# A GRU in sum-product form on one core: biases by DMA, first step's input products in scratch banks, last group's products made plainly

## The chip, the cores and the metric

One core of a Trainium2 chip runs the whole kernel. The metric is the device time of one execution in microseconds (us). The times below are medians; the profile is of one execution, with its own time. A difference of about 0.2% is what this measurement can tell from none.

## The reference

The input x has 64 sequences of 128 steps and 512 features; the state h starts from a second input (64 x 512). Cut to what matters:

```python
def step(h, inp):
    x_t, prop = inp
    comb = jnp.concatenate([x_t, h], axis=-1)
    z = jax.nn.sigmoid(comb @ Wz + bz)
    r = jax.nn.sigmoid(comb @ Wr + br)
    comb2 = jnp.concatenate([x_t, r * h], axis=-1)
    h_cand = jnp.tanh(comb2 @ Wh + bh)
    h_new = (1.0 - z) * h + z * h_cand
    h_next = jnp.where(prop, jnp.tanh(h_new @ Wp + bp), h_new)
    return (h_next, h_new)
...
x = x + ys        # ys: all the h_new
```

`prop` holds at every fourth step but the last. All is float32. Each gate's weight matrix has 512 rows for x_t (`wx` in the kernel) and 512 for h (`wh`).

## The kernel before, in words

**Layout.** The 64 sequences and two halves of the 512 features fill the 128 partitions: a state tile is 128 x 256 (`N` = 256), with half s on partitions 64s to 64s+63. A product with a 512 x 512 matrix is four calls of `product` (L196), one for each block k of 128 input features, each with one matmul for each half s (L187). A trace lists four records for one call. The activations, transposed for use as the stationary operand, come from `turn` (L205): four bf16 transposes on TensorE (L212), then one copy to SBUF on VectorE or ScalarE (L203).

**The recurrence.** One pass of the loop from L569 is a step: four products of h for R, four for Z; sigmoid of R, times h (`rh`, L602); `rh` transposed; Z's sigmoids and `keep` (L618); four products of `rh` for the candidate H; tanh, L648 and L653 to the new h; h transposed (L660, L662). At a chunk's end (`prop`) four products with Wp, a tanh and another transpose follow. The gates' PSUM slots (`slots`, in the tiles `rc` and `zp`) are seeded beforehand by ScalarE copies (`seed`, L392) with the input products and the bias of that step, which lie in `G`.

**The input products.** They do not depend on h and serve as fillers. A list `queue` holds single products; `fill(n)` (L400) issues the next n of them between the recurrence's own, and `read_out` (L407) issues the readers of those finished. How many go where is fixed by hand in `PLACES` (L537) and the numbers in the loop, by position u in a cycle of eight steps. Steps 0 to 7 are made plainly (`plain`, L411: 12 products a step, in two of the four scratch banks `q`, `r`, `a`, `x`, read by two VectorE additions with the bias, L419 and L424). From step 8 on, groups of four steps are made by a two-level fast matrix product (seven products of sums, each made of seven products of sums): 49 units a group of 128 x 192, in batches of two times seven (`batch`, L437), with sums of x and the final additions on GpSimd (L495, L499, L333 to L361) and reads by ScalarE and VectorE (L460 to L470). Two groups of 49 units are queued every eight steps (`batches`, L483). The weights' sums are made once, at the start: `sum_inner` (L318), `sum_outer` (L308), and in place in `wx` by L316 and L324. So `wx` no longer holds the plain weights later on, except in block k = 3. The last groups are 30 and 31 (steps 120 to 127).

**The start.** Each bias is loaded as a row to one partition (L109) and spread by matmuls with a row of ones (`spread`, L158) into `rc` and `zp`, from where VectorE copies it to `bias` (L168). `idle` (L177) issues matmuls of zeros. Then step 0's input products go straight to the gates' slots, with those of step 1 in between (L551 to L564).

**The queues.** TensorE, VectorE, ScalarE and GpSimd each take their instructions in program order. Loads are issued from SP's queue, some of the first ones from ScalarE's. A load may have to wait, on its issuing queue, for an earlier load's landing.

The functions that the diff touches, with the profile's line numbers:

Of the kernel before, what the change touches and what calls it, by code (L numbers as in the profile page):

```python
# [17 lines left out]
def kernel(  # L18
# [39 lines left out]
    FIRST = 2  # L58
    R, Z, H_ = range(3)
# [26 lines left out]

    bias_row = tt.rearrange("p a b c d e -> p (a b c d e)")[0:1, : 4 * H].rearrange(
        "p (i n) -> p i n", i=4
    )

# [17 lines left out]
    for i, b in enumerate((br, bh, bz, bp)):  # L108
        nc.scalar.dma_start(out=bias_row[:, i, :], in_=b.rearrange("(o n) -> o n", o=1))  # L109
    h_init = two.tile([P, N], F32, tag="h", name="h_init")  # L110
    new_xr(0)
    load_x(xr[0], 0, 2)
    for i in range(3):
        for k in (0, 2):
            load_w(wx[:, :, i, :], gates_in[i], k, k + 2, nc.sync if k == 0 else nc.scalar)
        if i == 0:
            for s in range(S):
                nc.scalar.dma_start(out=h_init[s * B : (s + 1) * B, :], in_=h0[:, ts(s, N)])
    for i in range(3):
        for k in (0, 2):  # L120
            load_w(wh[i], gates_in[i][D:, :], k, k + 2, nc.sync)
        if i == 0:
            load_x(xr[0], 2, 2, 2)
# [29 lines left out]
    bias = const.tile([P, C, 4, P], F32, name="bias")  # L153
# [3 lines left out]

    def spread(a, ps):  # L158
        for s in range(S):
            nc.tensor.matmul(  # L160
                ps[s * B : (s + 1) * B, :, :],
                lhsT=ones,
                rhs=bias_row[:, 2 * a : 2 * a + 2, ts(s, N)],
                start=True,
                stop=True,
            )
        for i in ((R, H_), (Z, 3))[a]:
            nc.vector.tensor_copy(bias[:, :, i, :], cut((slots[i] if i < 3 else slot_p)))  # L168
# [8 lines left out]
    def idle(n):  # L177
        for _ in range(n):
            nc.tensor.matmul(  # L179
                scratch[0][:B, :], lhsT=zeros[:, :B], rhs=zeros, start=True, stop=True  # L180
# [253 lines left out]

    MB = {}

    def batch(n, ms):  # L437
# [10 lines left out]
        def units(ps, j, start):  # L448
            return [lambda m=m: unit(ps, m, j, start) for m in range(2)]
# [4 lines left out]
        def end_1():  # L454
            MB[n] = mbp.tile([P, 2, 2, 3, P], F32, tag="mb", name=f"mb_{ms[0][0]}_{ms[0][1]}")
            for m, (g, i) in enumerate(ms):
                M[g, i] = MB[n][:, m]
            T2[n] = one.tile([P, 2, 3, P // 2], F32, tag="cx", name=f"cx_{ms[0][0]}_{ms[0][1]}")
            q1 = one.tile([P, 2, 3, P // 2], F32, tag="cq", name=f"cq_{ms[0][0]}_{ms[0][1]}")
            nc.scalar.copy(T2[n], x_ps)  # L460
            nc.scalar.copy(q1, q_ps)
            nc.vector.tensor_add(T2[n], r_ps, T2[n])  # L462
            nc.vector.tensor_add(blocks()[:, :, 0, 0], a_ps, q1)

        def end_2():
            q2 = one.tile([P, 2, 3, P // 2], F32, tag="cq", name=f"cq2_{ms[0][0]}_{ms[0][1]}")
            nc.scalar.copy(q2, q_ps)  # L467
            nc.vector.tensor_add(blocks()[:, :, 0, 1], r_ps, q2)  # L468
            nc.vector.tensor_add(blocks()[:, :, 1, 0], x_ps, q2)
            nc.vector.tensor_add(blocks()[:, :, 1, 1], q_ps, T2[n])  # L470
# [5 lines left out]
        seq[7] = (seq[7][0], end_1)  # L476
        seq[13] = (seq[13][0], end_2)
# [5 lines left out]
    def batches(g):  # L483
# [3 lines left out]
        ms = [(g, i) for i in (1, 2, 6, 5, 7, 3, 4)] + [(g + 1, i) for i in (1, 6, 2, 5, 3, 7, 4)]  # L487
        return sum((batch((g, n), ms[2 * n : 2 * n + 2]) for n in range(7)), [])
# [8 lines left out]
    def with_bias(g, i, v):  # L497
        m = M[g, i].rearrange("p b g u -> p b (g u)")
        nc.gpsimd.tensor_add(  # L499
            m, m, v.rearrange("p g u -> p (g u)").unsqueeze(1).to_broadcast([P, 2, 3 * P])  # L500
# [31 lines left out]
    def outer_c21(g):  # L532
# [7 lines left out]


    idle(10)
    spread(0, rc)
    turn_x(0, nc.vector)
    turn_x(1, nc.vector)
    spread(1, zp)
    nc.gpsimd.tensor_sub(bias_d, bias[:, 1, 0:3, :], bias0)
    idle(2)
    h = h_init
    hT = new_T("hT", "hT_init")  # L550
    first = [  # L551
        [lambda e=e, k=k: product(slots[e], xT[0][:, 0], wx[:, :, e, :], k) for k in ORDER]
        for e in range(3)
    ]
    second = plain(1)
    for e in range(3):

        queue.extend(second[4 * e : 4 * e + 4])
# [236 lines left out]
```

## Time and profile before

| | us |
|---|---|
| median of 3 runs | 1363.82 (1363.69 to 1363.88) |
| the profiled execution's own time | 1362.82 |
| its span, first to last instruction | 1361.0 |
| TensorE idle between 20 and 1300 us, by the waits | 2.7 |
| TensorE idle from 1300 us on, by the waits | 8.4 |

Of the chain that ended last, 98% lies on TensorE. Data moved by DMA in the first stretches, and the granted TensorE clock (1.00 is full):

| us | GB/s | share of DMA engines | clock |
|---|---|---|---|
| 2 to 4 | 133 | 0.61 | 1.00 |
| 4 to 6 | 250 | 0.91 | 1.00 |
| 6 to 8 | 398 | 1.04 | 1.00 |
| 8 to 10 | 346 | 1.06 | 1.00 |
| 10 to 11 | 331 | 1.09 | 0.74 |
| 12 to 13 | 385 | 1.05 | 0.50 |
| 13 to 14 | 385 | 1.05 | 0.55 |
| 14 to 15 | 387 | 1.06 | 1.00 |
| 20 to 25 | 318 | 1.09 | 1.00 |
| 25 to 30 | 267 | 1.10 | 1.00 |

How to read the rows quoted below. A row of the order of instructions gives start, duration, engine, line, operation, output and input tiles, shape and count; in brackets stands the idle time of the engine before it and what ended that. Matmul ends are modelled and overlap, so distances between starts tell more than durations. A row by windows gives the window, its length, the busy time and count of PE, PEld, DVE, ACT and POOL, then the granted clock, the share of the DMA engines and GB/s.

### The profile page before, as it was taken

The page shows a single profiled execution, that of the slowest core. Times are in us where ns is not written, and L with a number is a line of the kernel's source. Part 1 is how long each engine was busy: PE and PEld are TensorE (multiplying, and loading weights), DVE is VectorE, ACT ScalarE, POOL GpSimd, SP SyncE. Part 2 cuts the span into 40 slices and gives each one's busy share as a digit, 9 for nine tenths or more (in the row PEclk, how much of TensorE's full clock was granted, in tenths as well). Part 3 has the DMA queues.
Part 4 walks back from the last instruction along what each step waited for, and adds up shares of the span by engine and source line. Part 5 has one row for each costly group of instructions (what it writes and reads, how often), then busy time and mean ns, then how long its engine had stood idle before and what let it go on. Part 6 is the DMA issues. An engine that isn't in the chain of part 4 may idle for free.

```text
span 1361.0 us, 37468 instructions
## 1 busy us (share of the span) xinstructions
PE 1341.8 (99%) x15348; PEld 1033.1 (76%) x15348; DVE 686.0 (50%) x1875; ACT 630.6 (46%) x1857; POOL 935.7 (69%) x1140
## 2 busy tenths in 40 slices
PE   9999999999999999999999999999999999999996
PEld 6877777777777777777777777777777777777764
DVE  3255555555555555555555555555554555555543
ACT  1234544444544544444445444545445445444443
POOL 3448776778667768676787767777676686767740
PEclk9999999999999999999999999999999999999999
DMA  9011223121221222213222221222212212131010
GB/s 287 13 33 34 62 49 78 32 58 39 64 63 33 63 48 48 64 33 78 49 45 52 63 64 33 63 36 60 63 32 64 59 37 63 41 71 33 17 33 16
DMA packets 113572, 73.86 MB, mean 54 GB/s; under 512 B 61556, under 2 KB 109812, under 8 KB 113400
## 3 DMA queue, kind: packets, MB, share of 16 engines
q1 hardware_dynamic: 112336, 69.68, 22.6%
q8 instruction: 121, 1.98, 0.6%
q10 hardware_dynamic: 1064, 1.78, 0.4%
q14 instruction: 51, 0.42, 0.1%
HBM read 39.99 MB, written 16.78 MB: 42 GB/s over the span
## 4 chain that ended last, share of the span: by engine, by line
PE 98%; DVE 1%; ACT 0%; issue 0%; POOL 0%; DVEq 0%; POOLq 0%; ACTq 0%
PE rc L187 33%; PE zp L187 20%; PE scratch_q L187 11%; PE scratch_x L187 11%; PE scratch_r L187 10%; PE scratch_a L187 6%; PE turn L212 6%; PE scratch_q L179 0%; DVE h L653 0%; DVE turn L648 0%; ACT z L616 0%; PE rc L160 0%; ACT turn L647 0%; ACT xT L203 0%; ACT zp L617 0%
## 5 line engine op out<-in xcount | busy, mean ns | idle before, releaser
L187 PE MATMUL rc<-wh,rhT 128*64 128x256 f32 x2048 | 246.6, 381 | 2.0 <-ACT zp L617 2.0
L495 POOL TENSOR_TENSOR cp<-mb,mb 128x768 f32<-128x768 f32 x75 | 136.4, 1819 | 112.8 <-ACT rc L394 67.6
L187 PEld LDWEIGHTS rc<-wh,rhT 128*64 128x64 f32 x2048 | 158.9, 137 | 54.5 <-ACT zp L617 12.4
L187 PE MATMUL rc<-wh,hT 128*64 128x256 f32 x1536 | 183.1, 380 | 0.5 <-DVE hT L203 0.2
L187 PE MATMUL zp<-wh,hT 128*64 128x256 f32 x1536 | 183.2, 379 | 0.0
L203 DVE COPY rhT<-turn 128x256 uint16<-128x256 uint16 x256 | 96.7, 420 | 126.1 <-PE turn L212 126.1
L495 POOL TENSOR_TENSOR cp<-mb 128x768 f32<-128x768 f32 x45 | 81.9, 1819 | 108.2 <-ACT rc L394 107.0
L648 DVE TENSOR_TENSOR turn<-turn,z 128x128 f32<-128x128 f32 x256 | 75.5, 295 | 159.7 <-ACT turn L647 159.7
L187 PEld LDWEIGHTS zp<-wh,hT 128*64 128x64 f32 x1536 | 117.5, 137 | 47.3
L729 POOL TENSOR_TENSOR xr<-xr,h 128x256 f32<-128x256 f32 x127 | 92.8, 731 | 86.2 <-DVE h L653 85.2
L187 PEld LDWEIGHTS rc<-wh,hT 128*64 128x64 f32 x1536 | 111.6, 137 | 44.9 <-issue 1.0
L601 ACT ACTIVATE turn<-rc 128x128 f32<-128x128 f32 x256 | 55.4, 261 | 155.3 <-issue 84.2
L462 DVE TENSOR_TENSOR cx<-scratch_r,cx 128x384 f32<-128x384 f32 x105 | 58.6, 558 | 128.3 <-ACT cx L460 128.3
L203 ACT COPY hT<-turn 128x256 uint16<-128x256 uint16 x127 | 47.3, 373 | 155.8 <-PE turn L212 96.6
L495 POOL TENSOR_TENSOR mb<-mb,mb 128x768 f32<-128x768 f32 x60 | 109.4, 1824 | 14.2 <-DVE mb L470 14.2
L468 DVE TENSOR_TENSOR mb<-scratch_r,cq 128x384 f32<-128x384 f32 x105 | 58.6, 558 | 91.0 <-ACT cq L467 91.0
L394 ACT COPY rc<-cp 128x256 f32<-128x256 f32 x254 | 95.6, 376 | 11.6 <-POOL s L335 0.4
L616 ACT ACTIVATE z<-zp 128x256 f32<-128x256 f32 x128 | 49.2, 384 | 102.7 <-PE zp L187 100.8
L647 ACT ACTIVATE turn<-rc 128x128 f32<-128x128 f32 x256 | 56.7, 261 | 76.2 <-PE rc L187 76.2
L212 PEld LDWEIGHTS <-h 128*64 128x64 bf16 x1016 | 47.7, 109 | 50.5 <-DVE h L653 45.7
L394 ACT COPY zp<-cp 128x256 f32<-128x256 f32 x127 | 47.8, 377 | 74.5 <-DVE keep L618 74.5
L212 PE MATMUL turn<-ident,h 128*64 128x128 bf16 x1016 | 76.7, 227 | 5.4 <-DVE h L653 5.4
(152 smaller groups left out, 2960.4 us busy)
## 6 DMA issues: line engine op xcount, KB each, us to landing
xr<-in_x_dram SPq DMA_DIRECT2D x62, 256.0 KB, 4.2
out_dram<-xr SPq DMA_DIRECT2D x62, 256.0 KB, 3.4
xs<-in_x_dram SPq DMA_DIRECT2D x56, 256.0 KB, 4.3
wh<-in_L_cond_Wr_dram SPq DMA_DIRECT2D x2, 512.0 KB, 7.5
wh<-in_L_cond_Wz_dram SPq DMA_DIRECT2D x2, 512.0 KB, 8.9
wh<-in_L_cond_Wh_dram SPq DMA_DIRECT2D x2, 512.0 KB, 11.4
early<-in_x_dram SPq DMA_DIRECT2D x4, 256.0 KB, 13.4
wp<-in_L_cond_Wp_dram SPq DMA_DIRECT2D x1, 1024.0 KB
```

What stands on the lines that cost most here:

```text
L187: nc.tensor.matmul(ps[s * B : (s + 1) * B], lhsT=lhs, rhs=rhs(s), start=start, stop=True, skip_group_check=True,)
L203: (eng.copy if eng is nc.scalar else eng.tensor_copy)(dst, src)
L212: nc.tensor.transpose(pt[s * B : (s + 1) * B, w, :], words.rearrange("p (n w) -> p w n", w=2)[:, w, :], ident16,)
L394: nc.scalar.copy(cut(slots[i]), G[t][:, :, i, :])
L462: nc.vector.tensor_add(T2[n], r_ps, T2[n])
L468: nc.vector.tensor_add(blocks()[:, :, 0, 1], r_ps, q2)
L495: nc.gpsimd.tensor_add(dst, a, b)
L601: nc.scalar.activation(act_ps[c], slots[R][:, ts(c, P)], AF.Sigmoid)
L616: nc.scalar.activation(z, slots[Z], AF.Sigmoid)
L647: nc.scalar.activation(pc, slots[H_][:, ts(c, P)], AF.Tanh)
L648: nc.vector.tensor_mul(pc, pc, z[:, ts(c, P)])
L729: nc.gpsimd.tensor_add(xr[g][:, j, :], xr[g][:, j, :], h_new)
```

## The change

- The four biases are loaded by DMA on all 128 partitions (eight loads of 64 rows, in a layout by gate); the rows, the spreading matmuls and their copies go. Two of the loads come after the input weights on SP, the other two after the first weights for h.
- The first two steps of x are loaded in two halves, one as the first load on SP, the other as the first on ScalarE's queue. The initial state is loaded last on ScalarE's queue.
- `idle` makes fewer matmuls (6, 2 and 2 instead of 10 and 2), alternating between the halves of the partitions.
- Step 0's input products are made like those of step 1, in scratch banks, read with the bias and seeded into the slots.
- In step 3 the sums `sum_inner(5)` move from the end of the step to behind `keep`.
- Group 31 is made plainly: `plain_last` gives 48 products, and `reload` brings the overwritten blocks of the input weights back by nine loads at the end of step 118. All GpSimd work for group 31 goes. From step 119 on (`thin`), `TAIL` says how many fillers go where: none ahead of the candidate's products; two of Z's four products go behind the transposes of `rh`.

```diff
+    LAST = T // Q4 - 1
...
-    for i, b in enumerate((br, bh, bz, bp)):
-        nc.scalar.dma_start(out=bias_row[:, i, :], in_=b.rearrange("(o n) -> o n", o=1))
...
-    load_x(xr[0], 0, 2)
+    for s in range(S):
+        (nc.sync, nc.scalar)[s].dma_start(
+            out=xr[0][s * B : (s + 1) * B, 0:2, :], in_=x[:, 0:2, ts(s, N)]
+        )
     for i in range(3):
         for k in (0, 2):
             load_w(wx[:, :, i, :], gates_in[i], k, k + 2, nc.sync if k == 0 else nc.scalar)
-        if i == 0:
+    for s in range(S):
+        nc.scalar.dma_start(out=h_init[s * B : (s + 1) * B, :], in_=h0[:, ts(s, N)])
+
+    def load_bias(gates):
+        for i in gates:
             for s in range(S):
-                nc.scalar.dma_start(out=h_init[s * B : (s + 1) * B, :], in_=h0[:, ts(s, N)])
+                nc.sync.dma_start(
+                    out=bias_in[s * B : (s + 1) * B, i, :],
+                    in_=(br, bz, bh, bp)[i][ts(s, N)]
+                    .rearrange("(o n) -> o n", o=1)
+                    .broadcast_to([B, N]),
+                )
+
+    load_bias((0, 1))
     for i in range(3):
         for k in (0, 2):
             load_w(wh[i], gates_in[i][D:, :], k, k + 2, nc.sync)
         if i == 0:
+            load_bias((2, 3))
             load_x(xr[0], 2, 2, 2)
...
-    bias = const.tile([P, C, 4, P], F32, name="bias")
+    bias = bias_in.rearrange("p i (c n) -> p c i n", c=C)
...
+    def idle(n):
+        for i in range(n):
+            s = i % S
             nc.tensor.matmul(
-                ps[s * B : (s + 1) * B, :, :],
-                lhsT=ones,
-                rhs=bias_row[:, 2 * a : 2 * a + 2, ts(s, N)],
+                (rc, zp)[i // S % 2][s * B : (s + 1) * B, :, :],
+                lhsT=zeros[:, :B],
+                rhs=zeros,
                 start=True,
                 stop=True,
...
+    def plain_last():
+
+
+        def units(t, gates, first_k):
+            first, second = scratch[:2] if t % 2 == 0 else scratch[2:]
+            regions = (first[:, :N], first[:, N:], second[:, :N])
+            return [
+                lambda e=e, k=k: product(
+                    regions[e], xT[LAST][:, t % Q4], wx[:, :, e, :], k, k == 3 and e != Z
+                )
+                for k in first_k
+                for e in gates
+            ]
...
+        t0 = LAST * Q4
+        seq = [(u, None) for t in (t0, t0 + 1) for u in units(t, (R, Z, H_), (3,))]
+        for t in (t0, t0 + 1):
+            us = units(t, (R, Z, H_), (1, 0, 2))
+            seq += [(u, None) for u in us[:-1]] + [(us[-1], lambda t=t: end(t, (R, Z, H_)))]
+        for t, gates in ((t0 + 2, (R, Z, H_)), (t0 + 3, (R, Z)), (t0 + 3, (H_,))):
+            us = units(t, gates, (3, 1, 0, 2))
+            seq += [(u, None) for u in us[:-1]] + [(us[-1], lambda t=t, g=gates: end(t, g))]
+        return seq
+
+    def reload():
+
+        for k in (1, 0, 2):
+            for i in range(3):
+                load_w(wx[:, :, i, :], gates_in[i], k, k + 1, nc.sync)
...
-        ms = [(g, i) for i in (1, 2, 6, 5, 7, 3, 4)] + [(g + 1, i) for i in (1, 6, 2, 5, 3, 7, 4)]
-        return sum((batch((g, n), ms[2 * n : 2 * n + 2]) for n in range(7)), [])
+        ms = [(g, i) for i in (1, 2, 6, 5, 7, 3, 4)]
+        if g + 1 < LAST:
+            ms += [(g + 1, i) for i in (1, 6, 2, 5, 3, 7, 4)]
+        return sum((batch((g, n), ms[2 * n : 2 * n + 2]) for n in range(7) if 2 * n < len(ms)), [])
...
-        m = M[g, i].rearrange("p b g u -> p b (g u)")
+        m = M[g, i]
         nc.gpsimd.tensor_add(
-            m, m, v.rearrange("p g u -> p (g u)").unsqueeze(1).to_broadcast([P, 2, 3 * P])
+            m, m, v.unsqueeze(1).to_broadcast([P, 2, 3, P])
         )
...
-    idle(10)
-    spread(0, rc)
+    TAIL = (
+        ((4, 1, 0), (2, 1)), ((4, 1, 0), ()), ((4, 1, 0), ()), ((4, 1, 0), ()),
+        ((4, 1, 0), (2, 1)), ((4, 1, 0), ()), ((5, 1, 2), ()), ((3, 1, 0), ()), ((0, 0, 0), ()),
+    )
+
+
+    idle(6)
     turn_x(0, nc.vector)
+    idle(2)
     turn_x(1, nc.vector)
-    spread(1, zp)
+    idle(2)
...
+    both = [plain(0), plain(1)]
     for e in range(3):
-
-        queue.extend(second[4 * e : 4 * e + 4])
-        for n in range(4):
-            first[e][n]()
-            fill(1)
-        if e == 0:
+        for us in both:
+            queue.extend(us[4 * e : 4 * e + 4])
+        fill(4)
+        if e == H_:
+            read_out()
+            seed(R, 0)
+            seed(Z, 0)
+            seed(H_, 0)
+        fill(4)
+        if e == Z:
...
+        thin = t >= T - 9
+        if thin:
+
+            places, behind = TAIL[t - (T - 9)]
+            if t == T - 9:
+                assert not queue
+                queue.extend(plain_last())
+        if t == T - 10:
+
+            places = (4, 6)
+            assert len(queue) == 7
...
+        if t == T - 1:
+            seed(H_, t)
...
-        for k in ORDER[: 2 if last else K]:
+        for k in ORDER[: 2 if thin else K]:
             product(slots[Z], hT, wh[Z], k)
         rhT = new_T("rhT", f"rhT_{t}")
         for c in range(C):
             turn(rh, rhT, c, f"rhT_{t}", nc.vector)
-        if last:
-            for k in ORDER[2:]:
-                product(slots[Z], hT, wh[Z], k)
+            if thin:
+                product(slots[Z], hT, wh[Z], ORDER[2 + c])
...
         nc.vector.tensor_mul(keep, slots[Z], h)
+        if t == 3:
+            sum_inner(5, nc.vector)
+            sum_inner_1(5, nc.vector)
         seed(Z, t + 1)
...
-        fill(places[0])
+        if not thin:
+            fill(places[0])
...
-        fill(places[1] - 3 if places[1] > 6 else 4)
+        fill(places[0] if thin else places[1] - 3 if places[1] > 6 else 4)
...
-            fill(1)
+            fill(places[1] if thin else 1)
             turn(h, hT, 1, f"hT_{t}", nc.scalar)
-        fill(2 if places[1] > 6 else 1)
+        fill(places[2] if thin else 2 if places[1] > 6 else 1)
...
+        if t == T - 10:
+            reload()
```

## Prediction

> **What bounds the kernel now.** I read the page first, then busy time cut at the step boundaries (each step's first `rc<-wh,hT` matmul), then the order of instructions in the three places with idle TensorE: the start, step 3 and the end.
>
> ```profile
> span 1361.0 us, 37468 instructions
> ...
> PE 1341.8 (99%) x15348; PEld 1033.1 (76%) x15348; DVE 686.0 (50%) x1875; ACT 630.6 (46%) x1857; POOL 935.7 (69%) x1140
> ```
>
> TensorE is the bound nearly throughout. Its busy time is drawn out by pipelining, so I cost work by start-to-start distances: sixteen 128x256 records (four `product` calls) start 1.735 us before what follows them, so a product takes 0.434 us; a sum-product unit of 128x192 takes 0.325 (four records, 1258.12 to 1258.45); eight transposes 0.22. From about 108 to 1313 us nothing stops TensorE, and its work per step there is not changed. So only the start, step 3 and the tail count. The tail, by step (122, 123, 124, 127):
>
> ```profile
> 1303.63:1313.52 9.89, 9.71 (x117) 7.55 (x113) 5.60 (x15) 4.30 (x14) 6.42 (x5) 1.00 0.01 2
> 1313.52:1325.04 11.52, 8.88 (x89) 6.12 (x89) 4.91 (x14) 4.78 (x16) 6.20 (x5) 1.00 0.13 26
> 1325.04:1333.48 8.44, 6.46 (x64) 4.14 (x65) 2.99 (x10) 2.77 (x11) 0.40 (x1) 1.00 0.09 29
> ...
> 1350.35:1361.00 10.65, 5.77 (x56) 3.80 (x56) 2.76 (x9) 1.84 (x7) 1.06 (x2) 0.89 0.21 51
> ```
>
> The queue of input products runs dry in step 122; from 123 on the matmul count falls to 64 and each step is pure latency. Inside step 124:
>
> ```profile
> 1329.44 1.95 PE L187 MATMUL rc<-wh,rhT 128*64 128x256 f32 x16 [0.51 <-ACT zp L617]
> 1332.53 0.31 PE L212 MATMUL turn<-ident,h 128*64 128x128 bf16 x4 [1.14 <-DVE h L653]
> 1333.06 0.31 PE L212 MATMUL turn<-ident,h 128*64 128x128 bf16 x4 [0.22 <-DVE h L653]
> 1333.48 1.95 PE L187 MATMUL rc<-wh,hT 128*64 128x256 f32 x16
> ```
>
> The candidate product ends at 1329.44 + 1.735 = 1331.17; the state is back for its transpose 1.36 later and the next step starts 0.95 after that. 2.31 us hang on DVE and ACT; fillers there are free.
>
> **Part 1, the tail.** The last group's 49 sum-product units (49 x 0.325 = 15.9 us) become 48 plain products (48 x 0.434 = 20.8), 4.9 us more TensorE work, spread over steps 119 to 126 as 8, 5, 5, 5, 8, 5, 8 and 4. In these steps two Z products go behind the transposes of `rh`, in the form the last step already has. There R start to H start is 1350.35 to 1354.23 = 3.88 us, against 4.40 unfilled (1333.48 to 1337.88). H takes 1.735. Then four fillers (1.735) replace the 1.36 wait; the next step starts about 0.93 after the first transpose, because the copy on DVE (0.41) is then the last to come, and one 0.434 filler fits in it. A five-filler step is 3.88 + 1.735 + 1.735 + 0.03 + 0.93 = 8.3 us, as long as a step with none (8.44). By step, before against after: 118 (seven old units left, none between the transposes) 8.55, 9.1; 119 (with the 1.735 of the chunk-end product, two fillers and 0.84 from its transpose to the next step) 14.09, 11.8; 120 and 121 8.43, 8.44 against 8.3 each; 122 9.89, 8.3; 123 11.52, 11.8; 124 8.44, 8.3; 125 8.44, 9.4; 126 8.43, 7.9. Sums 86.2 and 83.3: **2.9 us gained**, and 127 as before. The ends: 4.9 if the transposed copy is ready when TensorE is (0.25 in each of eight steps), 0.2 if thinner Z cover costs 0.3 in each of nine steps. If the cover were gone altogether, the fillers would cost their 4.9.
>
> The nine reloads of the input weights (256 KB each, 2.36 MB) go on SP behind the load for group 30 and ahead of the output of step 119. No row shows this load alone. Near rows: 385 GB/s at the start with loads abreast, so 6 us; or 4.2 us for one 256 KB load, nine in a row 38 us. The first six products use the block that needs no reload, so the first reloaded piece is wanted late in step 119, the last at the end of 120, about 20 us after the issue. I take the abreast value: nothing. DVE reads of the plain products (four times 0.68 + 0.42 us) run under the R products of the following step; the removed reads and GpSimd additions (1.8 us each) weren't on the path.
>
> **Part 2, step 3.**
>
> ```profile
> 84.22 1.95 PE L187 MATMUL zp<-wp,hT 128*64 128x256 f32 x16
> 85.40 0.55 DVE L324 TENSOR_TENSOR wx<-wx 128x384 f32<-128x384 f32 x1
> 85.87 0.55 DVE L468 TENSOR_TENSOR mb<-scratch_r,cq 128x384 f32<-128x384 f32 x1
> 86.80 0.55 DVE L470 TENSOR_TENSOR mb<-scratch_q,cx 128x384 f32<-128x384 f32 x1
> 87.40 0.55 PE L187 MATMUL scratch_q<-tw,o 128*64 128x192 f32 x4 [1.23 <-DVE mb L470]
> ```
>
> TensorE was free at 84.22 + 1.735 = 85.96. The DVE reads that release the scratch bank stood behind the four `sum_inner(5)` operations (83.75 to 85.95). The change puts these four behind `keep`, where DVE was idle from 78.31 to 80.45; four at about 0.55 fill 2.2 us, and the next read comes at most 0.1 late, under the H products. The bank's reads then wait for ACT's copy (84.11 to 84.60) and end near 86.15: the stall shrinks from 1.44 to 0.2, **1.2 us gained**. Ends: 1.4, and 0 if the four take longer than here. The stalls at 94.24 and 104.57 (0.5 and 1.0 on DVE `rh`, behind ACT copies) stay.
>
> **Part 3, the start.**
>
> ```profile
> 7.77 2.68 SPq L98 DMA_DIRECT2D wh<-in_L_cond_Wr_dram  x2
> 9.50 1.07 PE L160 MATMUL zp<-tt,ones 1*64 1x512 f32 x4
> 10.51 0.69 PE L187 MATMUL rc<-wx,xT 128*64 128x256 f32 x1
> 13.49 0.59 PE L187 MATMUL rc<-wx,xT 128*64 128x256 f32 x1
> 25.15 1.89 PE L187 MATMUL zp<-wh,hT_init 128*64 128x256 f32 x15
> ```
>
> Removed: two `spread` pairs on TensorE (1.43 and 1.07 us), four DVE copies of 0.42, four row loads. The first x half lands 2.8 us after its issue, the other is issued 0.7 later on the same queue and lands after some 5; on two queues both should land near 3.5, not 6.6. The first wx load lands 5.6 after its issue, at 7.8; its queue comes to it 0.75 sooner, so I put it at 7.0. The x transposes end before (3.6 to 5.3, with 0.76 of DVE copies behind each). So products start at 7.0 instead of 10.51. The same 24 products follow, now in scratch banks for both steps; the DVE additions and ACT seeds that this adds for step 0 (0.69 + 0.42, then 0.38 each) lie under the last four products (1.735). If all else kept its distance (10.51 to 25.15, 14.64 us), step 0's Z products would start at 21.6.
>
> Two things hold that back. First the clock. The row: products take twice their later time until 13.49, three us after their start, although ten zero matmuls had run from 1.90 to 6.37. [...]
>
> Second the weights. A load waits for an earlier one's landing: the first wh load was held 3.9 us for wx. In the changed order both wh_R loads wait for the last wx halves, and eight bias loads of 64 KB (0.52 MB, 1.4 us at the 385 GB/s of 12 to 16 us) stand on SP ahead of and behind them, then x, then wh_Z. Summing from 3.5 MB moved near 12.7 us: wh_R lands near 17.4, wanted near 20.7; six issues of 0.65 bring wh_Z to 17.5 and its landing to about 22, under 22.7. With SP's later pace (1.3 MB from 17.6 to 22.5, 267 GB/s) it is 24.8. **2.4 us gained** (25.15 - 22.7); ends 0.3 and 3.8. GpSimd's `bias_d` waits for the bias of the candidate (11.15 before, near 19 now), and behind it nine `sum_inner` operations of 1.05; they had 7.3 us of waiting for DVE after them, which covers it. `with_bias` reads the bias in another layout, 1.83 us each; no row shows the new form, GpSimd is 69% busy, so I take nothing (a tenth more, 0.18 a piece, would still be hidden).
>
> **Sum.** 2.9 + 1.2 + 2.4 = 6.5 us. The profiled execution took 1362.8 (span 1361.0 and 1.8 around it) and would take 1356.3; the median is 1.0 above it, so 1363.8 - 6.5 = **1357.3**.
>
> **Rivals.** (a) The start is bound by loading: wh_Z at 24.8 leaves 0.3 of the 2.4, giving 1363.8 - 4.4 = 1359.4. For it: DMA share is full from 6 to 30 us. Against: TensorE never waited for wh before. (b) The tail doesn't pay: the 4.9 us of added products eat what the gaps gave, -3.6 or less in all, 1360.2. For it: all fillers sit behind H, none ahead of it. Against: step 127 shows the new form without a wait of 0.2. (c) Both at their good ends: 3.8 + 1.2 + 4.9, 1353.9. (d) Slower: the reload is late. TensorE takes instructions in order, so a filler waiting for weights stops the recurrence. If the nine came singly, 38 us against 20, some 15 to 18 us would be lost: 1363.8 - 6.5 + 15 = 1372. It decides once the reload takes over 26 us. Against it: wx itself, 3.1 MB, landed by 16.4.
>
> **Chances.** Forecast 0.56, (a) 0.20, (b) 0.09, (c) 0.10, (d) 0.05. About 0.2% (2.7 us) is what a measurement here can tell from no change; of (b) half stays within it, and of (a) a little. Faster 0.90, the same 0.06, slower 0.04. Range 1354.3 to 1360.8, from near (c) to past (b).
>
> **What would show it.** First product near 7.0, full clock between 10 and 14, step 0's Z near 22.7; TensorE waiting there for a DMA is (a). At step 3 no wait above 0.3 for `mb`. Step 119 to 126 near 11.8, 8.3, 8.3, 8.3, 11.8, 8.3, 9.4, 7.9; a filler waiting for wx is (d). A longer step between 108 and 1250 us would be a cost I haven't seen.

## The result and the profile after

The changed kernel takes 1357.64 us (median of 5 runs, 1357.26 to 1358.36) against 1363.82 (1363.27 to 1363.98): ratio 0.9956, 95% interval 0.9942 to 0.9969. The prediction said 1357.3. Its sum held; two of its three terms did not, and their errors cancelled: that the total came out so near is luck. The two profiled executions differ by 5.5 us of span (1361.0 and 1355.5), and where those lie can be read off.

The head of the page of the changed kernel:

```profile
span 1355.5 us, 37407 instructions
...
PE 1340.9 (99%) x15334; PEld 1015.3 (75%) x15334; DVE 685.5 (51%) x1866; ACT 627.5 (46%) x1851; POOL 913.1 (67%) x1111
```

TensorE is busy for 1340.9 us, nearly as long as before (1341.8), in a span 5.5 us shorter: what went is for the most part idle time, not work.

**The start.** TensorE's order of instructions in the changed kernel; lines have moved, `product` is L190, `turn` L215. The last row is of the kernel before:

```profile
9.48 3.68 PE L190 MATMUL scratch_q<-wx,xT 128*64 128x256 f32 x16 [2.66 <-DMA wx<-in_L_cond_Wr_dram]
12.95 2.07 PE L190 MATMUL scratch_a<-wx,xT 128*64 128x256 f32 x16
...
23.93 0.60 PE L190 MATMUL zp<-wh,hT_init 128*64 128x256 f32 x4
25.23 1.52 PE L190 MATMUL zp<-wh,hT_init 128*64 128x256 f32 x12 [0.69 <-DMA wh<-in_L_cond_Wz_dram]
26.57 0.39 PE L215 MATMUL turn<-ident,rh 128*64 128x128 bf16 x8
...
26.82 0.39 PE L212 MATMUL turn<-ident,rh 128*64 128x128 bf16 x7
```

Two waits for loads, in brackets, that the kernel before did not have: 2.66 us for wx_R (the input weights of gate R) and 0.69 for wh_Z (the weights of gate Z for h). By the distance between starts the second costs 0.9: from Z's first product to the transposes of `rh` it takes 2.64 us (23.93 to 26.57), and 1.72 before (25.10 to 26.82). Step 0's transposes of `rh` start 0.25 us earlier than before, of 2.4 predicted. I use this transpose as the mark of the start from here on.

**Step 3.** The same view; the last row is again of the kernel before:

```profile
83.97 1.90 PE L190 MATMUL zp<-wp,hT 128*64 128x256 f32 x16
85.86 0.55 PE L190 MATMUL scratch_q<-tw,o 128*64 128x192 f32 x4
...
88.31 1.90 PE L190 MATMUL rc<-wh,hpT 128*64 128x256 f32 x16
...
89.85 1.90 PE L187 MATMUL rc<-wh,hpT 128*64 128x256 f32 x16
```

No bracket stands on the second row, where 1.23 stood before. The next step starts at 88.31 instead of 89.85, 1.54 earlier; less the start's 0.25 that is 1.29.

**The tail.** The rows by windows for steps 122, 123, 124 and 127, as they were shown of before:

```profile
1299.33:1307.47 8.14, 8.07 (x84) 5.59 (x85) 4.06 (x12) 3.02 (x11) 0.72 (x1) 1.00 0.01 3
1307.47:1319.06 11.59, 11.52 (x121) 8.01 (x121) 4.63 (x13) 4.49 (x15) 0.73 (x1) 1.00 0.18 42
1319.06:1327.21 8.15, 8.08 (x85) 5.24 (x85) 3.42 (x11) 2.67 (x10) 0.69 (x1) 1.00 0.03 10
1344.16:1355.50 11.34, 5.83 (x56) 3.74 (x56) 3.11 (x10) 2.22 (x8) 1.06 (x2) 0.97 0.19 46
```

The first number behind each length is TensorE's busy time. In step 124 it was 6.46 of 8.44, and is 8.08 of 8.15: more work in a shorter step. Inside step 124 (from the candidate's products on) the order now reads:

```profile
1322.86 1.90 PE L190 MATMUL rc<-wh,rhT 128*64 128x256 f32 x16
1324.59 0.60 PE L190 MATMUL scratch_q<-wx,xT 128*64 128x256 f32 x4
...
1326.31 0.28 PE L215 MATMUL turn<-ident,h 128*64 128x128 bf16 x4
1326.42 0.60 PE L190 MATMUL scratch_r<-wx,xT 128*64 128x256 f32 x4
1326.86 0.28 PE L215 MATMUL turn<-ident,h 128*64 128x128 bf16 x4
1327.21 1.95 PE L190 MATMUL rc<-wh,hT 128*64 128x256 f32 x16
```

The waits of 1.14, 0.22 and 0.51 us are gone. Steps 118 to 126 take 8.90, 11.59, 8.15, 8.15, 8.14, 11.59, 8.15, 9.20 and 7.75, in sum 81.62 where it was 86.23: 4.61 us. Step 127, with what follows it, is longer: 11.34 against 10.65. With 0.04 between, the account closes: 0.25 + 1.29 + 0.04 + 4.61 - 0.69 = 5.5.

### The profile page after: what moved, and what is told of

Same layout as the page of the kernel before. It is cut to its first block, busy times and chain, and to the rows that moved or that the text cites. A ratio compares the mean times of both kernels' runs of the same rounds, so it can differ in the third digit from the quotient of the medians.

```text
span 1355.5 us, 37407 instructions
## 1 busy us (share of the span) xinstructions
PE 1340.9 (99%) x15334; PEld 1015.3 (75%) x15334; DVE 685.5 (51%) x1866; ACT 627.5 (46%) x1851; POOL 913.1 (67%) x1111
## 4 chain that ended last, share of the span: by engine, by line
PE 97%; DMA 1%; SPq 1%; ACT 0%; DVE 0%; issue 0%; DVEq 0%; ACTq 0%
PE rc L190 33%; PE zp L190 20%; PE scratch_q L190 11%; PE scratch_x L190 10%; PE scratch_r L190 10%; PE scratch_a L190 6%; PE turn L215 6%; DMA wx<-in_L_cond_Wh_dram 1%; DMA wh<-in_L_cond_Wz_dram 0%; SPq L94 0%; SPq L120 0%; ACT xT L206 0%; SPq L89 0%; ACT xT L276 0%; DVE rh L671 0%
## 5 line engine op out<-in xcount | busy, mean ns | idle before, releaser
L190 PE MATMUL rc<-wh,rhT 128*64 128x256 f32 x2048 | 246.1, 381 | 0.0
L546 POOL TENSOR_TENSOR cp<-mb,mb 128x768 f32<-128x768 f32 x72 | 131.0, 1820 | 106.9 <-ACT rc L397 64.6
L190 PEld LDWEIGHTS rc<-wh,rhT 128*64 128x64 f32 x2048 | 157.1, 137 | 54.7 <-ACT zp L685 9.2
L190 PE MATMUL zp<-wh,hT 128*64 128x256 f32 x1536 | 185.0, 379 | 0.0
L190 PE MATMUL rc<-wh,hT 128*64 128x256 f32 x1536 | 183.1, 380 | 0.5
L190 PEld LDWEIGHTS zp<-wh,hT 128*64 128x64 f32 x1536 | 115.3, 137 | 46.4
L190 PEld LDWEIGHTS rc<-wh,hT 128*64 128x64 f32 x1536 | 111.0, 137 | 45.5 <-issue 1.3
L546 POOL TENSOR_TENSOR mb<-mb,mb 128x768 f32<-128x768 f32 x58 | 105.7, 1823 | 11.9 <-DVE mb L519 11.9
L397 ACT COPY rc<-cp 128x256 f32<-128x256 f32 x256 | 96.4, 377 | 25.9 <-DVE cp L422 12.2
L725 DVE TENSOR_TENSOR h<-turn,keep 128x128 f32<-128x128 f32 x254 | 74.1, 292 | 15.4
L215 PEld LDWEIGHTS <-h 128*64 128x64 bf16 x1016 | 47.8, 109 | 45.4 <-DVE h L725 37.8
```

The lines of the kernel that those rows point to most:

```text
L190: nc.tensor.matmul(ps[s * B : (s + 1) * B], lhsT=lhs, rhs=rhs(s), start=start, stop=True, skip_group_check=True,)
L215: nc.tensor.transpose(pt[s * B : (s + 1) * B, w, :], words.rearrange("p (n w) -> p w n", w=2)[:, w, :], ident16,)
L397: nc.scalar.copy(cut(slots[i]), G[t][:, :, i, :])
L546: nc.gpsimd.tensor_add(dst, a, b)
L725: nc.vector.tensor_add(h_new[:, ts(c, P)], pc, keep[:, ts(c, P)])
```

## The experiments

Theory A: the start is bound by loads, by when they land and by the order in which SP's queue can issue them, and not by TensorE. Rival C: the start is bound by the sum of the bytes (6.4 MB stand ahead of step 0's mark), so that no order helps. Other rivals are put in words where they are expected. Every kernel is the changed one with the edit shown, cut to its main lines, unless another one is named. Behind "Measured" stand the median in us, the ratio to the kernel before and the ratio's 95% interval. "Before" was run beside each set; its medians were 1363.57 to 1364.41.

**The start alone.** The tail and step 3 as before.

```diff
-    LAST = T // Q4 - 1
+    LAST = T // Q4
...
-        thin = t >= T - 9
+        thin = False
```

> Only the start is changed (biases, x on two queues, step 0 by scratch banks); step 3 and the tail are as before. Theory A, loading order: the second Z product of step 0 waits for its weights until about 25.2 us, so the step after it starts 0.3 us earlier than before at most; time 1363.5, within 0.1% of before. Theory P, the working of the prediction: 2.4 us less, 1361.4. B, the start gives nothing because TensorE's clock rises later: then no wait for a load would stand in front of that Z product.

Measured: 1362.69 (11 runs), ratio 0.9993, interval 0.9984 to 1.0002. The start by itself gives nothing that can be told from zero. Rival B, no wait for a load in front of Z's products, is refuted by this execution. Its order of instructions shows the same wait again:

```profile
24.98 1.51 PE L190 MATMUL zp<-wh,hT_init 128*64 128x256 f32 x12 [0.66 <-DMA wh<-in_L_cond_Wz_dram]
26.33 0.39 PE L215 MATMUL turn<-ident,rh 128*64 128x128 bf16 x8
```

**The tail alone.** Start and step 3 as before.

```diff
-    load_bias((0, 1))
...
+    spread(0, rc)
```

> Only the tail is changed (last group plainly, reload); start and step 3 as before. A: steps 118 to 126 take 81.6 us instead of 86.2, the last one 11.3 instead of 10.7, so 3.9 us less, 1359.9. P: steps 118 to 126 take 83.3, 2.9 us less, 1360.9, with step 127 as before.

Measured: 1359.94 (7 runs), 0.9968, 0.9957 to 0.9979; span 1358.1. The start, which is the old one, came to its mark at 27.98 in this execution and at 26.82 in that of before: by the trace's clock records full clock was reached at 16.18 us, not at 13.90. Taking off these 1.16, the span is 4.06 shorter than before's, and 4.61 - 0.69 = 3.92 is what the changed kernel's tail and last step give.

**The sums of step 3 at their old place.**

```diff
-        if t == 3:
-            sum_inner(5, nc.vector)
-            sum_inner_1(5, nc.vector)
...
+        if t == 3:
+            sum_inner(5, nc.vector)
+            sum_inner_1(5, nc.vector)
```

> The changed kernel with the four operations of sum_inner(5) put back at the end of step 3. A and P alike: the wait of TensorE for mb in step 3 is back, 1.2 to 1.3 us longer than the changed kernel, 1358.9. Rival: other work of DVE takes the freed place and the time is the changed kernel's, 1357.6.

Measured: 1359.27, 0.9964, 0.9952 to 0.9977; span 1356.9, 1.4 more than the changed kernel's. The list of TensorE's waits from 30 to 1250 us shows the one that this edit brings back:

```profile
PE turn L215 <- DVE rh L671: 1.5, 2, 1.0
PE scratch_q L190 <- DVE mb L519: 1.2, 1, 1.2
```

In the changed kernel the same list has only the first row. From the start of step 3 to that of step 4 it takes 16.64 us here and 15.40 in the changed kernel. So the place of four VectorE operations is worth 1.24 us.

**The last seed behind the sigmoids.** In step 127 of the changed kernel ScalarE makes the candidate's seed copy in front of R's two sigmoids, because no earlier step seeds it any more:

```profile
1346.19 0.38 ACT L397 COPY rc<-cp 128x256 f32<-128x256 f32 x1 [1.71 <-PE rc L190]
1346.60 0.43 ACT L670 ACTIVATE turn<-rc 128x128 f32<-128x128 f32 x2
```

```diff
-        if t == T - 1:
-            seed(H_, t)
...
+        if t == T - 1:
+            seed(H_, t)
```

> The changed kernel with the last seed of H, in step 127, issued behind the two sigmoids of R on ACT. If that copy (0.38 us) in front of the sigmoids is what lengthens the last step (11.3 us for 10.7), the wait of 0.26 for rh goes and the last step is 0.3 to 0.4 us shorter, 1357.3. If the lengthening is all in the last transfer to memory, nothing changes, 1357.6.

Measured: 1357.78 (1356.17 to 1359.72), 0.9953, 0.9941 to 0.9966; span 1354.6. In its trace the copy stands behind, and the 0.26 us wait for `rh` is gone:

```profile
1345.81 0.43 ACT L668 ACTIVATE turn<-rc 128x128 f32<-128x128 f32 x2 [1.67 <-PE rc L190]
1346.27 0.38 ACT L397 COPY rc<-cp 128x256 f32<-128x256 f32 x1
```

From the step's first product to the last issue it takes 7.40 us; the changed kernel 7.80, the one before 7.48. The five kernels of this document with the copy behind have 7.39 or 7.40, the seven with the new tail and the copy in front 7.79 or 7.80. So the 0.4 is shown by the traces; in the medians it is lost in their spread.

The start of this kernel is that of the changed one, instruction for instruction, and its execution shows how much chance there is in it:

```profile
8.18 3.68 PE L190 MATMUL scratch_q<-wx,xT 128*64 128x256 f32 x16 [1.43 <-DMA wx<-in_L_cond_Wr_dram]
11.65 3.18 PE L190 MATMUL scratch_a<-wx,xT 128*64 128x256 f32 x16
...
26.19 0.39 PE L215 MATMUL turn<-ident,rh 128*64 128x128 bf16 x8
```

The products start 1.3 us sooner than in the changed kernel, and the mark comes only 0.38 sooner: full clock came at 14.23 instead of 13.30.

**Biases on ScalarE's queue.** SP then issues wh_R and wh_Z right behind wx; x's later slices follow wh_Z.

```diff
-                nc.sync.dma_start(
+                nc.scalar.dma_start(
                     out=bias_in[s * B : (s + 1) * B, i, :],
...
+    load_wh(R)
+    load_bias((0, 1))
+    load_wh(Z)
+    load_x(xr[0], 2, 2, 2)
```

> The changed kernel with the bias loads on ACT's queue and both wh_R and wh_Z loads right behind wx on SP's. Theory A, issue order on SP: the loads no longer pause between 12 and 22 us, wh_Z has landed by about 21 and the wait of 0.7 us for it goes; products still start near 9.4, so 0.7 us less than the changed kernel, 1356.9. Rival C, bytes: the DMA engines carry all they can, wh_Z lands near 25 as before and the time is 1357.6; or the earlier wh loads slow wx and it is 1358 or more.

Measured: 1358.70, 0.9963, 0.995 to 0.9977. The wait for wh_Z is gone, but x, now behind it, is waited for:

```profile
25.28 0.42 PE L218 MATMUL turn<-ident,xr 128*64 128x128 bf16 x8 [2.06 <-DMA xr<-in_x_dram]
25.50 3.44 PE L193 MATMUL zp<-wh,hT_init 128*64 128x256 f32 x16
28.67 0.67 PE L218 MATMUL turn<-ident,rh 128*64 128x128 bf16 x8
```

The second row is new too: sixteen records in 3.17 us (25.50 to 28.67) that take 1.73 otherwise. The granted clock of 26 to 28 us is 0.50: on top of the wait these records cost 1.44.

**Products in the order in which wx_R was thought to land.** ScalarE's half of wx_R landed 3.5 us before SP's in the changed kernel, so its two blocks go first.

```diff
+        order = (2, 3, 0, 1) if t < 2 else ORDER
...
-            for k in ORDER
+            for k in order
```

> The changed kernel with the products of steps 0 and 1 taken in the order of landing: first the blocks of ScalarE's loads (k = 2 and 3), then those of SP's. Products start near 6.2 instead of 9.5. A: nothing is gained, because the Z products of step 0 still wait for wh_Z until about 25: time 1357.6, and the wait for wh_Z grows from 0.7 to 2 or 3 us. P, a start bound by TensorE's own work: 2 to 3 us less, 1355.

Measured: 1357.33 (1356.43 to 1360.53), 0.9959, 0.9947 to 0.9972. In this execution SP's half landed first and the products started at 8.94; the mark stands at 26.61. No gain.

**Both of these together.**

> The two foregoing edits together. A: products start near 6.2, wh_Z lands near 21 as step 0's Z products come up, so the transposes of rh in step 0 come about 3 us earlier than in the changed kernel (26.6 to 23.6): 1354.6. C, bytes: no gain beyond 0.7, 1357.

Measured: 1359.89 (1356.76 to 1361.52), 0.9972, 0.9961 to 0.9984. The profiled execution is the fastest of them. Here ScalarE's half did come first:

```profile
6.35 1.97 PE L193 MATMUL scratch_q<-wx,xT 128*64 128x256 f32 x8
...
20.56 1.95 PE L193 MATMUL rc<-wh,hT_init 128*64 128x256 f32 x16 [1.65 <-ACT rc L400]
24.22 0.42 PE L218 MATMUL turn<-ident,xr 128*64 128x128 bf16 x8 [1.72 <-DMA xr<-in_x_dram]
...
26.17 0.42 PE L218 MATMUL turn<-ident,rh 128*64 128x128 bf16 x8
```

Products started 3.1 us earlier and the mark came 0.4 earlier. The rest went into waits of 1.65 us for a seed (VectorE's addition ahead of it waited 2.60 for a bias) and 1.72 for x.

**The same with the late seed**, as a candidate for the best version.

> The two edits at the start together, and the last seed of H behind the sigmoids of R. A: 3 us at the start and 0.4 at the end, 1354.2, under both kernels. C: 1356.8.

Measured: 1358.33, 0.9963, 0.995 to 0.9975. SP's half came first again, products started at 9.58, and both waits stayed (1.21 and 1.03); the mark stands at 28.05.

**Fewer and larger loads.** With the late seed and the biases on ScalarE's queue, like the two kernels after it.

```diff
-    for i in range(3):
-        for k in (0, 2):
-            load_w(wx[:, :, i, :], gates_in[i], k, k + 2, nc.sync if k == 0 else nc.scalar)
+    for k in (0, 2):
+        load_w(wx[:, :, R, :], Wr, k, k + 2, nc.sync if k == 0 else nc.scalar)
+    load_w(wx[:, :, Z, :], Wz, 0, 4, nc.sync)
+    load_w(wx[:, :, H_, :], Wh, 0, 4, nc.scalar)
...
+    load_w(wh[R], Wr[D:, :], 0, 4, nc.sync)
```

> The changed kernel with the last seed copy of the last step behind R's sigmoids, and with fewer and larger loads at the start: wx_R in halves on both queues, wx_Z whole on SP's, wx_H whole on ScalarE's, then wh_R whole on SP's, x's later slices, wh_Z whole, and all biases on ScalarE's queue. Theory A (the start is set by the order of issue and by what an issue waits for): no issue on SP's queue waits for the landing of wx_H any more, so TensorE waits neither for wh_Z nor for x; first products at about 9.3 us, step 0's turn of rh at 25.5 to 25.9 us (26.6 in the changed kernel), 0.7 to 1.1 us less, with 0.4 from the seed copy: 1356.5. Theory C (the bytes set it): turn of rh still at 26 us or later, 1357.2.

Measured: 1360.43 (1357.25 to 1361.29), 0.9969, 0.9958 to 0.9981. No load of weights is waited for any more after wx_R, but a bias is (VectorE's addition ahead of the seed waits 3.40 us for it), and the granted clock falls again, to 0.50 from 25 to 28 us:

```profile
9.49 3.68 PE L188 MATMUL scratch_q<-wx,xT 128*64 128x256 f32 x16 [2.93 <-DMA wx<-in_L_cond_Wr_dram]
...
24.96 3.54 PE L188 MATMUL rc<-wh,hT_init 128*64 128x256 f32 x16 [2.18 <-ACT rc L395]
```

A failed here: it named 25.5 to 25.9 for the mark, which came at 30.29.

**Small loads first.** Biases and the initial state stand first on ScalarE's queue.

```diff
+    load_bias(R)
+    load_x(xr[0], 0, 2)
+    load_w(wx[:, :, R, :], Wr, 0, 4, nc.sync)
+    load_bias(Z)
+    load_w(wx[:, :, Z, :], Wz, 0, 4, nc.sync)
+    load_bias(H_)
...
+    load_w(wx[:, :, H_, :], Wh, 0, 4, nc.scalar)
```

> As the kernel above, but the small loads (two biases of each gate, h's initial value) stand first on ScalarE's queue, wx_H whole behind them, and SP's queue has x, wx_R whole, wx_Z whole, wh_R, x's later slices, wh_Z, wh_H. Theory A: wx_R has the engines nearly to itself and lands at about 7.3 us, so products start there, no wait for a bias, x or wh_Z follows, and step 0's turn of rh stands at about 23.5 us: about 1354.2. Theory C: the start moves earlier by what wx_R gains, and a later load gives it back; turn of rh at 26 us or later, 1357.2.

Measured: 1359.01 (1356.31 to 1359.55), 0.9959, 0.9947 to 0.9972. Now there is no late wait but 0.76 us for wx_Z; the loads run without a pause (share of the DMA engines 1.03 or more from 6 to 30 us). And the mark is no earlier:

```profile
10.33 3.28 PE L184 MATMUL scratch_q<-wx,xT 128*64 128x256 f32 x16 [2.44 <-DMA wx<-in_L_cond_Wr_dram]
...
26.96 0.39 PE L209 MATMUL turn<-ident,rh 128*64 128x128 bf16 x8
```

The loss is ahead of the first product. A's 7.3 us for wx_R was 3 us wrong. The trace keeps sixteen landing marks for each of these loads, and I count a load as landed at the last: here fifteen of wx_R's stand at 7.7 to 9.2 us and the last at 10.3.

**All weights in one queue**, so that wx_H no longer runs beside wx_R. The edit is against the kernel just above.

```diff
-    load_w(wx[:, :, H_, :], Wh, 0, 4, nc.scalar)
+    load_w(wx[:, :, H_, :], Wh, 0, 4, nc.sync)
```

> As the kernel with the small loads first, but wx_H stands behind wx_Z on SP's queue and not beside them on ScalarE's: x, wx_R, wx_Z, wx_H, wh_R, x's later slices, wh_Z, wh_H in one row, the small loads on the other queue. If the start is set by which bytes come first (wx_H's megabyte shared the engines with wx_R, which therefore landed only after 10 us there), wx_R lands at about 7.5 us, every later load comes in its turn ahead of its use, and step 0's turn of rh stands at about 24 us (27.0 there, 26.6 in the changed kernel): about 1354.7 with the seed copy's 0.4. If the bytes as a whole set it, one of the later loads is waited for instead and the turn of rh stays at 26 us or later: 1357.2.

Measured: 1358.74 (1358.63 to 1361.62), 0.9962, 0.9949 to 0.9974. wx_R landed at 11.04, later still, and the mark stands at 27.86. SP's queue shows the reason for what follows wx_R:

```profile
2.27 0.60 SPq L94 DMA_DIRECT2D wx<-in_L_cond_Wr_dram  x1
9.19 0.38 SPq L94 DMA_DIRECT2D wx<-in_L_cond_Wz_dram  x1
11.05 0.37 SPq L94 DMA_DIRECT2D wx<-in_L_cond_Wh_dram  x1
```

wx_Z was held for the landing of a bias load of 64 KB, until 9.19, and the engines ran dry (share 0.47 from 8 to 10 us). Even so wx_R, alone but for 0.5 MB in small loads, took 8.8 us: fifteen of its landing marks stand at 7.4 to 8.9, the sixteenth at 11.0. The simple form of my theory, that whichever load is put first comes early, fell with this.

The traces show what the holds end with. In them each issue names one of eight semaphores, and the loads take these in turn, over both queues. In the first 40 us of the kernel before and of the changed one (50 pairs of loads, one after the other on the same semaphore) none was issued before the load that had its semaphore last had landed, and 26 were issued within 0.15 us of that landing. By that count a load waited for the eighth load before it: here wx_Z for the bias (issued at 9.19), and wx_H for wx_R (11.04, issued at 11.05).

**Two megabytes fewer.** The first two steps take wx_R for all three gates, so wx_Z and wx_H can come behind all the rest; the values are then others, TensorE's instructions the same.

```diff
+    for i in (Z, H_):
+        for k in (0, 2):
+            load_w(wx[:, :, i, :], gates_in[i], k, k + 2, nc.sync)
...
+                regions[e], xT[g][:, i], wx[:, :, R if t < 2 else e, :], k, k == ORDER[0] and e != Z
```

> The changed kernel with 2 of the 6.4 MB that stand ahead of step 0's turn of rh moved behind it: the products of the first two steps use wx_R for all three gates (so their values are not the reference's), and wx_Z and wx_H are loaded behind wh_H. TensorE's instructions are the same. If loading sets the start and TensorE's own work does not: wx_R alone lands at about 7 us, no wait for wh_Z follows, and step 0's turn of rh stands at about 24 us, as the prediction had it for the changed kernel itself (2.4 us less). If the start were set by TensorE's clock or by its own order of work, the turn of rh would stay near 26 us. The time as a whole, if wx_Z and wx_H come soon enough for step 2: about 1355.2; if not, up to 1357.6.

Measured: 1358.63 (4 runs), 0.9957, 0.9942 to 0.9972; a wait of 1.64 us for wx_H, now loaded late, stands at 31.67, so only the start counts:

```profile
8.99 3.68 PE L193 MATMUL scratch_q<-wx,xT 128*64 128x256 f32 x16 [2.44 <-DMA wx<-in_L_cond_Wr_dram]
12.46 2.64 PE L193 MATMUL scratch_a<-wx,xT 128*64 128x256 f32 x16
...
25.75 0.39 PE L218 MATMUL turn<-ident,rh 128*64 128x128 bf16 x8
```

The wait for wh_Z is gone, as loading as the cause has it, and the mark is 0.82 us earlier than in the changed kernel. But the products start only 0.5 us earlier, for SP's half of wx_R landed 7.4 us after its issue (7.9 in the changed kernel) with two of the 6.4 MB out of the way. So neither form of the loading theory was right: not the sum of the bytes (C), nor the order alone (A).

**What the set shows.** In every execution of the new start but one the products waited for the half of wx_R that landed last, and started at 8.2 to 11.1 us. From there to the mark three things add up: TensorE's own work, the slow clock, and the waits for later loads. The work at full clock is 14.26 us (6.90 for the four groups of sixteen records ahead of the transposes of `h_init`, and 7.36 from there on, taken from the kernel with two megabytes fewer, which has no later wait). While the clock is slow sixteen records take 3.47 us (9.48 to 12.95 in the changed kernel) for the 1.73 of later (14.85 to 16.58), so half of the stretch from the first product to full clock is lost; full clock is where the trace's clock records have it. The later waits are taken from the distances between starts.

| kernel | products start | lost to the slow clock | later waits | mark |
|---|---|---|---|---|
| changed | 9.48 | 1.9 | 0.9 | 26.57 |
| the same start, late seed | 8.18 | 3.0 | 0.7 | 26.19 |
| the start alone | 9.19 | 1.8 | 1.1 | 26.33 |
| two megabytes fewer | 8.99 | 2.5 | 0 | 25.75 |
| small loads first | 10.33 | 1.4 | 0.9 | 26.96 |
| all weights in one queue | 11.08 | 1.6 | 0.9 | 27.86 |
| biases on ScalarE's queue and the other order | 6.35 | 1.8 | 3.8 | 26.17 |

With 14.26 each row adds up to its mark within 0.1 us. So the start is bound by the landing of wx_R, the clock and the later loads together, and what a kernel gained in one of them it lost in another. The clock's part is chance as far as is known: with the start of the changed kernel it was 1.4 (the sums of step 3 at their old place) to 3.0. None of the versions beats the changed kernel by more than the spread.

## Why the prediction was right, and where it was not

**Part 3, the start: wrong, 0.25 us for 2.4.** The step that failed is "so I put it at 7.0", the landing of the first load of wx. I took SP's half of the kernel before (5.6 us from issue to landing) and moved it by the 0.75 us that its issue came sooner. In the changed kernel that half took 7.9 us and landed at 9.4. The DMA engines' share was 0.95 from 4 to 6 us and 1.02 to 1.04 from 6 to 10, and by the GB/s of the slices some 2.3 MB had moved by 9.4, of which wx_R and x's first slices are 1.3. ScalarE's half, issued 0.05 earlier, took 4.4. So 2.5 of the 3.5 us by which products were to start sooner were never there. In the kernel before both halves were there by 8.1 us, by the landing marks: with the new order of issues the second came later, not sooner. One difference is that ScalarE's half of wx_Z was issued at 6.06 us there and at 2.15 here; no run takes this alone.

The second failed step is the landing of wh_Z "about 22, under 22.7"; it came at 25.2. That is the mechanism of rival (a), and its value for the gain, 0.3, is what was found, though wh_Z made only 0.9 of the loss. What I had priced as bytes was a queue. SP's part of the chain of work that ended last, in the changed kernel:

```profile
2.93 11.79 DMA wx<-in_L_cond_Wh_dram
...
14.74 0.37 SPq L94
...
18.92 1.33 SPq L94
...
20.30 4.89 DMA wh<-in_L_cond_Wz_dram
...
25.23 1.52 PE zp L190 x12
```

wh_R's second half waits for wx_H to land, six small issues follow one by one, then wh_Z's first half is issued at 18.9 (wh_Z was predicted for 17.5) and its second, the one waited for, at 20.3; it lands 4.9 us later. While SP waits, the engines have little to do, by windows:

```profile
12.00:14.00 2.00, 2.00 (x16) 1.13 (x14) 0.00 (x0) 0.00 (x0) 0.00 (x0) 1.00 0.81 215
14.00:16.00 2.00, 2.00 (x22) 1.32 (x20) 0.00 (x0) 0.00 (x0) 0.00 (x0) 1.00 0.84 218
16.00:18.00 2.00, 2.00 (x22) 1.32 (x20) 0.00 (x0) 0.00 (x0) 0.00 (x0) 1.00 0.71 190
```

The last two numbers are the share of the DMA engines and GB/s; before they were 1.05 to 1.09 and 284 to 387 there. I summed bytes at the full rate through a stretch where loads were held.

The third is the clock. "Three us after their start" is a misreading: the table ahead of the prediction has 0.55 for 13 to 14 us, and the trace's clock records have half clock from 10.48 to 13.90, 3.4 us. Ahead of that stretch the clock was full, from 7.07 to 10.48, and it fell just as the products began. The 22.7 of the sum stands 1.1 above the 21.6 that the distances give, for the clock, and no run shows that term; step 0's first Z product started at 23.93. In the changed kernel the first record of full clock is at 13.30, 3.8 us after the first product (the granted clock of the rows shows 1.00 until then, but sixteen records take 3.47 us there, twice the later 1.73). So the clock cost 0.2 us more than before, for the 1.1 of the sum. Between executions with the new start the stretch was 2.7 to 6.0 us; since half of it is lost, that is a spread of 1.7 us, and with the late seed it took back most of what the earlier products gave.

Against the prediction the start then adds up: 2.5 lost at wx_R and 0.9 at wh_Z; 0.9 got back at the clock, and 0.35 because the work from the first product to the mark is shorter than I had it (14.26 us at full clock, 14.6 in the kernel before). That is 2.15 of the 2.4.

**Part 2, step 3: right.** 1.2 predicted, 1.29 measured, and 1.24 when it was undone alone.

**Part 1, the tail: right mechanism, one term too small.** 2.9 predicted for steps 118 to 126, 4.6 measured. The term that was mis-sized is the length of a step with five fillers: 8.3, worked out as 3.88 + 1.735 + 1.735 + 0.03 + 0.93. It measures 3.80 + 1.73 + 1.72 + 0.90 = 8.15. The other steps came 0.15 to 0.2 shorter than predicted in the same way. So nine steps make 1.7 us. I had taken the pieces from rows of the kernel before in which TensorE still waited a little at each handover; with work in between, the list of TensorE's waits has a single one left from 1250 us to the last step, of 0.2. The alternative that I gave, 4.9 "if the transposed copy is ready when TensorE is", is near what happened. The reload, rival (d), took 2.7 to 5.4 us for each of the nine loads, the last landing 9.1 us after the first issue, and nothing waited for it.

**"127 as before": wrong, by 0.7.** 0.32 of it is the seed copy in front of R's sigmoids (7.80 against 7.48 us to the last issue); undone, 7.40. I had not followed where the last `seed(H_)` goes when its old place is cut off. The other 0.37 is the last store, 3.54 us from its issue to the end against 3.17. The other traces show that this is chance: it takes 3.12 to 3.48 in those with the new tail, and 3.33 with the old tail and the new start.

**The sum.** Predicted 2.4 + 1.2 + 2.9 = 6.5; measured 0.25 + 1.29 + 0.04 + 4.61 - 0.69 = 5.5 in the two profiled executions and 6.2 between the medians. The errors of -2.15, +0.1, +1.7 and -0.7 leave 1.0 in the former. Most of the rest is that the profiled execution of before lies 1.0 below its median and that of the changed kernel only 0.4. So the number 1357.3 was right by luck; the steps that gave it were right for step 3 and, in mechanism, for the tail. What I had costed at nothing between, the bias in another layout on GpSimd among it, cost nothing: the stretch from step 4 to 117 changed by 0.04. Rival (b), that the tail would not pay, is refuted; of rival (a) the start is confirmed and the total is not.

**What stays open.** Why the second half of wx_R needs 6.6 to 8.0 us from its issue, although the 1.3 MB of wx_R and x's first slices would take 3.4 at 385 GB/s. The sixteen landing marks narrow it down: the first half's lie close together (5.2 to 5.9 us in the changed kernel), the second's are spread from 6.7 to 9.4, with the last three at 9.0 or later. So the wait is for a few late parts. What holds these back no run shows. Small loads are a candidate: from 6 to 11 us with all weights in one queue, the small ones moved 0.45 MB at 31.8% of the engines' time and the weights 0.65 MB at 37.4%. An order without small loads near wx_R was not tried.

## What to carry to other kernels

Cost a start by the order of issues on each queue, and write beside every load which earlier landing holds it (in the 50 pairs counted here that of the eighth load before it; with all weights in one queue a bias of 64 KB held the 1 MB of wx_Z until 9.19 us); a sum of bytes at the full rate is only a floor (3.4 us for wx_R and x's first slices, whose last part landed 6.6 to 8.0 after its issue). An edit that lets the first product start sooner is worth nothing until each later load, and the clock, have been checked against the new times (products at 6.35 for 9.48 us brought the mark 0.4 earlier). In this tail, which hung on latency, filler work between dependent steps cost less than its own time plus the old handovers, since these handovers ended sooner than the filler did (4.9 us of added work by my estimate, steps 118 to 126 shorter by 4.61, and the waits of 1.14, 0.22 and 0.51 in step 124 gone); but follow every small operation whose old place is cut off, for it lands in front of something.

## What was not expected of the hardware

- Two equal loads of 512 KB, issued within 0.05 us of each other on two queues, landed 4.4 and 7.9 us later. Which queue's came first differed between executions: ScalarE's in the changed kernel and in the one whose products began at 6.35, SP's in two others with the same first loads. In all ten executions with these loads it was the one whose issue ended first (at 2.10 to 2.13 us, the other's at 2.30 to 2.39).
- After a wait of TensorE of 2.06 us (biases on ScalarE's queue) or 2.18 us (fewer and larger loads), both near 24 us, the granted clock was 0.50 and the next sixteen records took 3.2 to 3.4 us instead of 1.73, a price of 1.4 to 1.7 on top of the wait; with waits of 1.65 and 1.72 us (the biases there and the other order together) it was 1.00 from 22 to 30 us, and the sixteen records behind the second took 1.72. With the old start the clock fell too, at 10.48 us (9.35 with the tail alone), and there no single wait of TensorE between its first matmul, at 1.90 us, and the fall was over 0.84. What the fall goes by no run shows.
- The kernel before, unchanged, ran between 1362.36 and 1365.78 over the sets, and its 47 executions beside the experiments fall into three groups by their mean granted clock, without overlap: 0.998, 1362.36 to 1363.01; 0.997, 1363.14 to 1364.42; 0.999 or 1.000, 1365.18 to 1365.78. The kept trace is of the first group. In it half clock stands from 10.48 to 13.90, and with the old start in the tail-alone kernel (0.997) from 9.35 to 16.18, so the spread of this kernel looks like the clock at its start; no trace of the third group was kept.
